# Deformable layer: the grid is added to the 7x7 block's positions by VectorE in place of GpSimd

## The chip, the core and the metric

The kernel runs on one core of a Trainium2 chip. A core has five engines with instruction streams of their own: TensorE (PE in the profile; PEld are its weight loads), VectorE (DVE), ScalarE (ACT), GpSimd (POOL) and SyncE (SP), which here issues most DMAs. They work in parallel and wait for each other by semaphores. Each engine takes its instructions in order, so an instruction that waits holds back all those behind it. The metric is the device time in microseconds of one execution, the median of several.

## What is computed

Four layers on a batch of 8 images of 384 channels, 32x32, all f32, each added to its input: a state-space layer, a deformable convolution, a second state-space layer with an MLP, and a displacement with a small Gaussian filter. The change is in the second. There the 384 normalized channels are split into three blocks of 128, with kernels of 3x3, 5x5 and 7x7. Each block computes offsets by an ordinary convolution, samples its input at the displaced positions with bilinear weights, tap by tap, and mixes channels by a 1x1 convolution:

```python
def deform_block(x, ow, ob, dw, pw, pb, K):
    offsets = conv2d(x, ow, ob, pad)             # 2*K*K channels: dy, dx of each tap
    out = deform_depthwise(x, offsets, dw, K, pad)
    return conv2d(out, pw, pb, 0)
...
    py = gy[None] + ky_k + o_k[:, 0]             # in deform_depthwise, for each tap:
    px = gx[None] + kx_k + o_k[:, 1]             # grid + place of the tap + offset
    acc = acc + sample(py, px) * w_k[None, :, None, None]
```

The 7x7 block has 49 taps, so 98 rows of 1024 positions for each sample. The addition of `gy + ky` and `gx + kx` to these 98 rows is the piece of work that the change touches.

## The kernel before

`tile_net` (line 1725) runs the layers one after another. The deformable layer is `deform_fast` (line 925): it covers about 3060 to 6000 us of the profiled span. If the largest offset, in units of a radius, is too large (`far`), a slower general version (`deform_layer`) computes the layer again; the flag is read at line 1735.

**Units and slots.** For each sample the taps of the three blocks are grouped into sets of up to four (`QUADS`: 3, 7 and 13 sets). Each set is done in two halves of the image rows, which gives 46 units for each sample: units 0 to 5 are the 3x3 block, 6 to 19 the 5x5 block, 20 to 45 the 7x7 block. The loop at line 1007 goes over slots, one unit each, and pipelines four steps of different units in one slot u:

- `positions` (line 1378, DMA at line 1384 on SP) for unit u+4, when it is a first half: it reads the positions of the set's taps from DRAM (`posd`) and broadcasts them over the partitions into `fpyx`. `fpyx` has two buffers, one for the two halves of a set.
- `unit_hats` (line 1389, ScalarE) for unit u+2: bilinear weights in x (`fhx`, lines 1400 and 1406, first half only) and in y (`fhy`, lines 1413 and 1418). Two buffers each.
- `unit_dve` (line 1422, VectorE) for unit u+1: weights the transposed input by the taps (`fxk`, line 1436) and multiplies the hats (`fsm`, line 1453), both from two SBUF operands.
- `unit_pe` (line 1470, TensorE) for unit u: matmuls that accumulate in PSUM (`wacc`, line 1483).

**Everything else goes into the slots by hand.** `block_steps` (line 1058) places the other steps of a block with `put(slot, place, fn)`. A place such as "dve0" is ahead of the slot's units on an engine, "dve1" after them. The order on TensorE, VectorE and ScalarE is the order written out (`manual_schedule`, line 1006). GpSimd and SP are not in that list.

**The 7x7 block's positions.** Its offsets come from a convolution that is split into three parts of matmuls (`fir`, line 1124), in slots 0 to 13 of the sample. `fir_take` (line 1140) puts the even and odd columns into the tile `fpos` (98 x 1024). In slot 14, at "dve0", `fir_end` (line 1151) follows:

```python
def fir_end():
    pos = s["pos"][:used]
...
    nc.gpsimd.tensor_tensor(pos, pos, grid[:used], ALU.add)
    s["posd"] = self.dram.tile([2 * K2, L], F32, name="fposd", tag=f"posd{K}")
    nc.sync.dma_start(out=s["posd"], in_=pos)
```

It takes the largest and smallest offset of each row (lines 1156 and 1157, VectorE), adds the grid in place (line 1158, GpSimd), and stores the sum to DRAM (line 1160, SP). `grid` is a constant of the layer: the setup adds the taps' places to it (line 953). The first set of the 7x7 block, units 20 and 21, has a single tap. Its positions are loaded in slot 16, and its hats are due in slots 18 and 19, its products in 19 and 20. On SP its load stands behind line 1160 and reads what that DMA writes.

The 3x3 and 5x5 blocks add their grid as they take the offsets out of PSUM (line 1184, VectorE) and don't use line 1158.

Of the kernel before, what the change touches and what calls it, by code (L numbers as in the profile page):

```python
# [10 lines left out]
ALU = mybir.AluOpType  # L11
# [80 lines left out]
class Net:  # L92
# [965 lines left out]
    def block_steps(self, b, g, first, put, weights, src, dst):  # L1058
        nc, K = self.nc, KS[g]
        K2, pad = K * K, K // 2  # L1060
        n, st, cols = CONV[K]
        ow, ob, obk, grid, _ = self.f[K]
# [53 lines left out]
        used = width * n  # L1116
# [34 lines left out]
        def fir_end():  # L1151
            pos = s["pos"][:used]
            for e, (op, sign) in enumerate(((ALU.max, 1.0), (ALU.min, -1.0))):
                k = 8 * b + 2 * g + e
                fc = self.far[:used, k : k + 1]
                nc.vector.tensor_reduce(fc, pos, AX.X, op)  # L1156
                nc.vector.tensor_scalar(fc, fc, sign / RAD[K], None, ALU.mult)
            nc.gpsimd.tensor_tensor(pos, pos, grid[:used], ALU.add)  # L1158
            s["posd"] = self.dram.tile([2 * K2, L], F32, name="fposd", tag=f"posd{K}")
            nc.sync.dma_start(out=s["posd"], in_=pos)  # L1160

# [150 lines left out]
        elif g == 1:  # L1312
            t = first[b, 0] - 12
            for i in range(6):
                put(t + i, "pe1", conv, 0, K2 * i // 6, K2 * (i + 1) // 6)
            put(t + 6, "dve0", offsets, 0)
        else:
            t = first[b, 0]
            put(t - 1, "dve1", fir_sum)
            k = 0  # L1320
            for part, pieces in enumerate((4, 5, 5)):
                nw = K * len(FIR[part])
                for i in range(pieces):
                    where = "pe0" if t + k in (first[b, 0], first[b, 1]) else "pe1"
                    put(t + k, where, fir, part, nw * i // pieces, nw * (i + 1) // pieces)
                    k += 1
                put(t + k, "dve0" if part else "act0", fir_take, part)
            put(t + k, "dve0", fir_end)
# [486 lines left out]
```

## Time and profile before

| | |
|---|---|
| device time, median of 3 runs | 9660.02 us (9657.92 to 9662.58) |
| profiled execution | 9658.17 us, of which the span is 9656.4 us |
| mean granted TensorE clock | 0.941 |
| TensorE busy, matmuls | 8491.1 us (88%) |
| VectorE busy | 8114.4 us (84%) |
| ScalarE busy | 6482.8 us (67%) |
| GpSimd busy | 6012.0 us (62%) |
| GpSimd, line 1158 | 8 instructions |
| VectorE, line 1156 (largest and smallest of `fpos`) | 16 instructions, 1.21 us each |
| SP, line 1160 (`fpos` to DRAM) | 8 DMAs of 392 KB |
| SP, line 1384 (`fpyx` from DRAM), sets of four taps | 640 DMAs of 256 KB |
| SP, line 1384, sets of one tap | 24 DMAs of 1024 KB |
| from 3284.8 to 5817.9 us, first to last line 1158: TensorE, VectorE, ScalarE busy | 2270.1, 1944.0, 1896.8 of 2533.1 us |

The span is the time from the first to the last instruction of the profiled execution. Busy shares are averages over layers with different limits, so they don't say what bounds the deformable layer; that is read from who waits for whom there, and from the instructions in order of time. An engine's idle time is put down to what ended it. In this layer GpSimd has no work but line 1158 after its setup, the last of which starts at 3096.7 us.

### The profile page before, as it was taken

How to read it: one execution, taken by the hardware profiler on the slowest of the kernel's cores; microseconds unless marked ns; L12 is line 12 of the kernel's file. 1: busy time of each engine (PE TensorE's matmuls, PEld its weight loads, DVE VectorE, ACT ScalarE, POOL GpSimd, SP SyncE). 2: the span in 40 equal slices, each digit the busy share in tenths (PEclk: the TensorE clock that was granted, in tenths of full speed). 3: DMA queues.
4: the chain of work that ended last, by engine and by line, in shares of the span. 5: the costliest groups of instructions: out<-in, count | busy, mean ns of one | idle time of the engine just before them, and what ended most of it. 6: DMA issues, size and time to landing. Idle time of an engine off the chain costs nothing. (4 is left out here: it accounts for less than half of the span.)

```text
span 9656.4 us, 87414 instructions
## 1 busy us (share of the span) xinstructions
PE 8491.1 (88%) x27891; PEld 4504.2 (47%) x27916; DVE 8114.4 (84%) x8879; ACT 6482.8 (67%) x10148; POOL 6012.0 (62%) x3803
## 2 busy tenths in 40 slices
PE   7898888888886898898898898589999999999987
PEld 3333333333332677677677677233443434434333
DVE  6989999999996678778778778699999999999983
ACT  5666666666663677777777777567777776777750
POOL 6888888888895101101101101599999999999974
PEclk8999999999998999999999999799999999999998
DMA  2211211121121233333333332224333233322336
GB/s 73 81 58 46 83 55 48 61 75 52 49 80 46 71 81 79 87 81 79 87 82 78 87 82 68 85 76 132 95 96 93 89 119 109 96 89 91 110 106 128
DMA packets 566095, 791.97 MB, mean 82 GB/s; under 512 B 244274, under 2 KB 397266, under 8 KB 542072
## 3 DMA queue, kind: packets, MB, share of 16 engines
q1 hardware_dynamic: 513400, 779.99, 27.7%
q10 hardware_dynamic: 52224, 6.30, 0.4%
q8 instruction: 223, 3.65, 0.2%
q14 instruction: 248, 2.03, 0.1%
HBM read 716.49 MB, written 69.66 MB: 81 GB/s over the span
## 5 line engine op out<-in xcount | busy, mean ns | idle before, releaser
L433 POOL TENSOR_TENSOR db<-du,bc 128x1024 f32<-128x1024 f32 x1536 | 3608.3, 2354 | 424.5 <-DVE hs L443 232.0
L443 DVE TENSOR_TENSOR_SCAN da<-da,db 128x1024 f32<-128x1024 f32 x1272 | 2912.5, 2290 | 200.0 <-ACT da L428 149.4
L474 PE MATMUL y<-hs,ident 128*128 128x512 f32 x5184 | 2608.1, 639 | 385.1 <-DVE hs L457 246.1
L428 ACT ACTIVATE da<-dt,na 128x512 f32<-128x512 f32 x3072 | 2120.2, 691 | 915.4 <-DVE hs L457 684.6
L474 PEld LDWEIGHTS y<-hs,ident 128*128 128x128 f32 x5184 | 1020.3, 204 | 1870.9 <-issue 1137.8
L1158 POOL TENSOR_TENSOR fpos<-fpos,fgrid 98x1024 f32<-98x1024 f32 x8 | 244.1, 30508 | 2504.8 <-DVE far L1156 2504.8
L1483 PE MATMUL wacc<-fsm,fxk 128*128 128x221 f32 (+34 forms) x10624 | 1645.1, 313 | 98.8 <-DVE fsm L1453 96.0
L1483 PEld LDWEIGHTS wacc<-fsm,fxk 128*128 128x128 f32 x10624 | 1554.8, 194 | 241.2 <-DVE fsm L1453 162.3
L457 DVE TENSOR_TENSOR hs<-da,bc 128x1024 f32<-128x1024 f32 x1272 | 1557.9, 1225 | 117.2 <-PE y L474 12.8
L1453 DVE TENSOR_TENSOR fsm<-fhy,fhx 128x170 f32<-128x170 f32 (+42 forms) x3216 | 1170.7, 428 | 468.6 <-PE wacc L1483 312.5
L1413 ACT ACTIVATE fhy<-fpyx,cell 128x416 f32<-128x416 f32 (+9 forms) x1280 | 645.5, 576 | 373.3 <-DVE fsm L1453 373.3
L1436 DVE TENSOR_TENSOR fxk<-fxt,fwk 128x1024 f32<-128x1024 f32 (+1 forms) x688 | 787.2, 1180 | 10.1 <-ACT fxt L1226 10.1
L443 DVE TENSOR_TENSOR_SCAN hs<-da,db 128x1024 f32<-128x1024 f32 x264 | 602.4, 2282 | 71.8 <-PE y L474 28.6
L454 POOL TENSOR_TENSOR hs<-hs,bc 128x1024 f32<-128x1024 f32 x264 | 621.8, 2355 | 36.8 <-ACT st L449 36.3
L461 POOL TENSOR_TENSOR hs<-hs 128x512 f32<-128x512 f32 x480 | 609.0, 1269 | 3.6 <-DVE hs L457 3.6
L557 PE MATMUL ps_m<-hid,wm 128*128 128x512 f32 x1152 | 536.8, 611 | 29.0 <-ACT hid L550 24.3
L535 PE MATMUL ps_h<-t,wm 128*128 128x512 f32 x1152 | 539.2, 606 | 14.5 <-DVE x L564 14.4
L1418 ACT ACTIVATE fhy<-fhy,cols 128x1344 f32<-128x1344 f32 (+10 forms) x368 | 530.6, 1442 | 12.0
L401 POOL TENSOR_TENSOR dt<-dt,sp_e 128x512 f32<-128x512 f32 x192 | 243.8, 1270 | 356.6 <-DVE sp_e L393 356.6
L449 ACT COPY st<-da 128x2 f32<-128x2 f32 x624 | 97.8, 157 | 505.5 <-DVE hs L457 504.1
L1135 PE MATMUL ps_off<-fxn,fow 128*98 128x465 f32 (+10 forms) x896 | 386.6, 579 | 0.0
L1400 ACT ACTIVATE fhx<-fpyx,cell 128x544 f32<-128x544 f32 (+8 forms) x640 | 380.0, 666 | 0.0
(203 smaller groups left out, 10086.3 us busy)
## 6 DMA issues: line engine op xcount, KB each, us to landing
bc<-bcd SPq DMA_DIRECT2D x256, 1024.0 KB
fpyx<-fposd SPq DMA_DIRECT2D x640, 256.0 KB
wm<-in_w SPq DMA_DIRECT2D x96, 768.0 KB
x<-x SPq DMA_DIRECT2D x71, 768.0 KB
winr<-in_win SPq DMA_DIRECT2D x192, 192.0 KB
x<-in_x SPq DMA_DIRECT2D x40, 768.0 KB
fpyx<-fposd SPq DMA_DIRECT2D x24, 1024.0 KB
wm<-in_wout SPq DMA_DIRECT2D x48, 384.0 KB
```

Of the source, the lines that this page charges most:

```text
L428: nc.scalar.activation(da[:, i, :], s["dt", j], AF.Exp, scale=na[:, j, n : n + 1])
L433: nc.gpsimd.tensor_tensor(db, du, s["bc"][m][:, 0], ALU.mult)
L443: nc.vector.tensor_tensor_scan(h1, da1, db1, 0.0, ALU.mult, ALU.add)
L454: nc.gpsimd.tensor_tensor(s["hs", m], s["hs", m], c, ALU.mult)
L457: nc.vector.tensor_tensor(hs, s["da", m], c, ALU.mult)
L461: nc.gpsimd.tensor_tensor(hs[:, 0, :], hs[:, 0, :], hs[:, 1, :], ALU.add)
L474: nc.tensor.matmul(s["y"], self.ident, s["hs", m][:, i, :], start=first and i == 0, stop=k == NU - 1 and i == n - 1,)
L535: nc.tensor.matmul(ps, s["w1"][:, k, f * P : (f + 1) * P], s["t"][:, k, :], start=(k == 0), stop=(k == G - 1))
L1413: nc.scalar.activation(hy[:, at : at + (yb - ya) * W], pyx[:, 0, ya * W : yb * W], AF.Abs, bias=bias)
L1436: nc.vector.tensor_tensor(t[:, :n], x, wk[:, j : j + 1, :].to_broadcast([P, n, P]), ALU.mult)
L1453: nc.vector.tensor_tensor(self.sub(sm, at, [(r * w, n), (w, r), (1, w)]), self.sub(hy, hy_at[by] + xa, [(r * W, n), (W, r), (1, w)]), self ...
L1483: nc.tensor.matmul(a[:, ya - 4 * o : yb - 4 * o, xa:xb], k, self.sub(sm, sm_at[by], [(w, yb - ya), (1, w)]), start=False, stop=False,)
```

## The change

The addition in `fir_end` is issued to VectorE's stream instead of GpSimd's. Operands and result are the same: `fpos` plus the first 98 rows of `grid`, in place. In VectorE's order it stands behind the four instructions of lines 1156 and 1157 and ahead of slot 14's products. The store of line 1160 then waits for VectorE. Nothing else is changed.

```diff
@@ -1155,7 +1155,7 @@
                 fc = self.far[:used, k : k + 1]
                 nc.vector.tensor_reduce(fc, pos, AX.X, op)
                 nc.vector.tensor_scalar(fc, fc, sign / RAD[K], None, ALU.mult)
-            nc.gpsimd.tensor_tensor(pos, pos, grid[:used], ALU.add)
+            nc.vector.tensor_tensor(pos, pos, grid[:used], ALU.add)
             s["posd"] = self.dram.tile([2 * K2, L], F32, name="fposd", tag=f"posd{K}")
             nc.sync.dma_start(out=s["posd"], in_=pos)
```

## The prediction

> **What bounds the kernel now.** I read the page first, for the instruction that the change moves. It has three columns after the shapes: busy time in all and mean ns of one; idle time of its engine before it; what ended that idle time.
>
> ```profile
> span 9656.4 us, 87414 instructions
> ...
> L433 POOL TENSOR_TENSOR db<-du,bc 128x1024 f32<-128x1024 f32 x1536 | 3608.3, 2354 | 424.5 <-DVE hs L443 232.0
> ...
> L1158 POOL TENSOR_TENSOR fpos<-fpos,fgrid 98x1024 f32<-98x1024 f32 x8 | 244.1, 30508 | 2504.8 <-DVE far L1156 2504.8
> ```
>
> The reader is to see the odd one: the same operation on the same 1024 elements a partition takes 2354 ns in line 433 and 30508 ns in line 1158. Eight of them, one for each sample, all in the deformable layer. GpSimd has nothing else to do there, so its 244 us cost nothing by themselves. The question is who waits for the result, and what makes it so slow.
>
> Next the waits, in the window of the deformable layer (3000 to 6200 us): total, times, longest. The first answer is SP's own queue, the second that of the engines.
>
> ```profile
> SPq L1160 <- POOL fpos L1158: 300.5, 8, 44.0
> ```
>
> ```profile
> DVE fsm L1453 <- ACT fhy L1418: 153.0, 33, 16.4
> ...
> ACT fhx L1400 <- DMA fpyx<-fposd: 138.0, 8, 17.5
> ...
> PE ps_t L1221 <- DVE frep L1215: 137.0, 10, 16.6
> ```
>
> Eight times SP stands at line 1160, the DMA that writes the finished positions to DRAM, until GpSimd is done. Eight times ScalarE waits some 17 us for positions to come back. VectorE and TensorE show a 16 us wait each, about as often. To see whether that is one stall or several, I read the timeline round the first of them (start, length, engine, line).
>
> ```profile
> 3284.80 2.35 DVE L1436 TENSOR_TENSOR fxk<-fxt,fwk 128x1024 f32<-128x1024 f32 x2
> 3284.84 30.50 POOL L1158 TENSOR_TENSOR fpos<-fpos,fgrid 98x1024 f32<-98x1024 f32 x1 [185.29 <-DVE far L1156]
> ...
> 3305.18 1.05 ACT L1226 COPY fxt<-ps_t 128x512 f32<-128x512 f32 x2
> ...
> 3309.22 3.31 DVE L1453 TENSOR_TENSOR fsm<-fhy,fhx 128x234 f32<-128x234 f32 x12
> ...
> 3312.44 0.69 DVE L1436 TENSOR_TENSOR fxk<-fxt,fwk 128x512 f32<-128x512 f32 x1
> ...
> 3315.37 0.31 SPq L1160 DMA_DIRECT2D fposd<-fpos  x1
> 3318.37 15.38 SPq L1384 DMA_DIRECT2D fpyx<-fposd  x9
> 3323.41 1.15 ACT L1400 ACTIVATE fhx<-fpyx,cols 128x1024 f32<-128x1024 f32 x1 [17.17 <-DMA fpyx<-fposd]
> ...
> 3329.18 1.76 DVE L1453 TENSOR_TENSOR fsm<-fhy,fhx 128x256 f32<-128x256 f32 x3 [16.05 <-ACT fhy L1418]
> 3329.99 2.03 ACT L1413 ACTIVATE fhy<-fpyx,cols 128x384 f32<-128x384 f32 x4
> ...
> 3331.43 1.94 PE L1221 MATMUL ps_t<-ident,frep 128*128 128x128 f32 x8 [16.21 <-DVE frep L1215]
> ```
>
> It is one stall. ScalarE runs out of work at 3306.24 (it starts at 3323.41 after 17.17 us idle), VectorE at 3313.13, TensorE soon after; all wait for the chain add (ends 3315.34), write to DRAM (3.0 us to the next issue), broadcast back (5.0 us more), hats. Asking the waits in a short window round each of the eight gives ScalarE waits of 17.2, 17.5, 17.1, 17.3, 17.4, 17.3, 17.3 and 16.8 us.
>
> Last, busy time by stretch (PE, PEld, DVE, ACT, POOL, then granted clock, DMA share, GB/s):
>
> ```profile
> 3285.00:3313.00 28.00, 24.81 (x180) 24.00 (x180) 28.00 (x63) 16.10 (x24) 28.00 (x1) 0.94 0.00 1
> 3313.00:3331.00 18.00, 2.17 (x13) 1.37 (x13) 1.95 (x5) 7.53 (x11) 2.34 (x1) 0.67 0.48 139
> 3331.00:3360.00 29.00, 22.05 (x105) 16.81 (x105) 23.50 (x43) 27.87 (x42) 0.00 (x0) 0.85 0.48 127
> 3360.00:3400.00 40.00, 35.59 (x214) 34.33 (x215) 38.16 (x84) 34.13 (x47) 0.00 (x0) 0.91 0.36 80
> ```
>
> VectorE is busy for all of 3285 to 3313 while the add hangs, and the add ends 2.2 us after VectorE falls silent (3315.34 less 3313.13), about the length that line 433 has for one. So the add seems to wait until VectorE has no work left, and VectorE has none left because the positions are late: the stall makes itself.
>
> **What the Trainium skill says.** "SBUF — State Buffer", section "Who interferes with whom": VectorE and GpSimd share a pair of ports, and "A DVE instruction with two SBUF inputs contends with a GpSimd instruction that reads SBUF". Lines 1436 and 1453, which fill that stretch, both have two SBUF inputs. The trace agrees, with 30.5 us against 2.35 us, and goes further: the add is not let in between two VectorE instructions either. "GPSIMD Engine Reference", section "Performance versus the Vector engine", gives 2293 ns for an add of 2048 f32 elements on VectorE, so an estimate of 1.15 us for 1024; the trace has 1.22 us for line 1436 (1217 ns on average in 3284 to 5818 us, same types, two SBUF inputs), and I use that.
>
> **The change, part by part.**
>
> Removed: eight GpSimd adds. Nothing else of GpSimd runs in this layer after its setup (last 3096.70, next of another line 6134.19), so that alone is worth nothing.
>
> Added: eight VectorE adds of 98x1024, 1.22 us each. The bounds are 1.15 (the page) and 1.38 (twice the 0.69 us of line 1149, which reads PSUM, for 512). They follow line 1157 in VectorE's written-out order, ahead of lines 1436 and 1453 of the same slot. VectorE is full there, so all of it is on the path: everything up to 3313 shifts by 1.22. It is 9.8 us in all.
>
> Moved: the DMA of line 1160. It now waits for VectorE, at 3284.88 + 1.22 = 3286.1 instead of 3315.37. Behind it in SP's queue stands line 1384 for the first unit of the 7x7 block (unit 20 of the sample). Its data are in DRAM at 3286.1 + 3.0 = 3289.1. Its buffer comes free when ScalarE ends the hats of unit 17, at 3290.00 + 1.89 = 3291.9, or 3293.1 with the shift. Then 5.0 us of transfer: 3298.1. ScalarE needs it at 3306.24. The wait of 17.2 us goes, with 8.1 us to spare. The next load (unit 22) needs the buffer that unit 19's hats free at 3303.7 and has until the hats of unit 22, which move from 3334.37 to some 3318, so it isn't late.
>
> What is late next: ScalarE does the hats of unit 20 (5.7 us in the trace, 3323.41 to 3329.15) from 3306.24 to 3312.0 and one pair of copies (1.05) to 3313.0. The hats of unit 21 then need a buffer that VectorE frees at the end of unit 19's products, 3309.22 + 3.31 + 1.22 = 3313.75. In the trace they start at 3329.99. The gain is 3329.99 less 3313.75, 16.2 us. VectorE itself starts unit 20 at 3314.35 in place of 3329.18 (14.8 earlier), but its wait of 2.9 us for ScalarE at line 1240 comes next (sums, which move with ScalarE), so ScalarE's 16.2 stands. TensorE's wait for line 1215 lies in the same gap and is not counted again.
>
> Sum: the other samples' ScalarE waits differ little, so 137.9 in all (the eight above) less 8 x 1.22 = 9.8 gives 128; by the one worked out in full 8 x 16.2 = 130. I take 129. From the profiled execution, 9658.17 (span 9656.4), that is 9529; its distance to the median of 9660.02 is 1.9 us, within the three runs' spread. I say 9529.
>
> One thing could add to it. The granted clock is 0.67 in the stall and 0.85 and 0.91 in the 70 us after, against 1.00 in stretches from 3400 to 3646. Without a stall it may stay up. In those 70 us VectorE and ScalarE are nearly full (23.5 and 27.9 of 29, then 38.2 of 40), so I cost it at nothing; if half of TensorE's extra time counted (22.05 x 0.15 + 35.59 x 0.09 = 6.5 us), it would be 3.3 us for each sample, 26 us in all.
>
> **The rivals.**
>
> *More than that: the clock.* The stall's cold clock was on the path after it. For it: the 0.85. Against: who is full there. Time: 9529 - 26 = 9503; with all of the 6.5 us, 9477.
>
> *Less: another wait takes its place.* TensorE's busy time is 90% of 2533 us in this layer, and VectorE waits 312.5 us for line 1483 in all (320 waits, none over 5.6 us). If TensorE sets the pace of the units after the pivot, or the positions collide with the next sample's input, which is loaded just after them, half of the gain goes: 9658 - 65 = 9593. Against it: the mean DMA share is 0.32 there, and TensorE, starved from 3315 on, has no backlog at the pivot.
>
> *Nothing: the load isn't released earlier*, because SP still stands behind something else, or the reload is bound by its buffer. Then only the added work remains: 9658 + 10 = 9668. Against it: the buffer's release at 3291.9 is read from the trace, and SP issues nothing between 3271.3 and 3315.37.
>
> *Slower: the price belongs to the operands, not to the engine.* If 98 partitions or this pair of tiles make any engine slow, VectorE takes 30.5 us, in order, with all its products behind it. Unit 19's products then end at 3312.53 + 30.5 = 3343.0 and the pivot moves from 3329.99 to 3343: 13 us for each sample, 9762. It decides from a VectorE add of about 17.5 us on (3329.99 less 3312.53); 20 us would be 9678. Against it: VectorE reads the same fpos tile of 98x1024 in 1.21 us at line 1156, and GpSimd did 98x1024 with one input in 2.85 us at line 953.
>
> **How the numbers follow.** Forecast 0.76 (9529), more 0.10 (9503), less 0.08 (9593), nothing 0.03 (9668), slower 0.03 (9762). The forecast's own range comes from 14.8 to 17.3 us per sample: 9520 to 9540. The range to hold 8 in 10 reaches into the clock's case and half of the way to the halved gain: 9503 to 9562; beyond it lie about half of the cases more and less, and the last two, some 15 in 100. A change under 0.2%, about 19 us, couldn't be told from none. Forecast, more and less lie beyond it on the fast side (0.94), nothing within it (0.03), slower 0.03.
>
> **What would show it.** Right: VectorE has a row for line 1158 of 98x1024 at about 1220 ns; SP's wait at line 1160 falls from 300 us to a few times the shift; ScalarE's wait of line 1400 for fpyx falls from 138 to near 0; VectorE's for line 1418 from 153 to some 25; the interval of two samples' line 1158 falls from 361.9 us (2533.1 / 7) to about 346; the clock stays above 0.9. Wrong: a wait for fpyx of over 5 us left at the start of the 7x7 block, an add longer than 2 us, or a new wait on TensorE of over 5 us in each sample.

## The result, and the profile after

| | before | after |
|---|---|---|
| median, device time | 9661.19 us (9657.92 to 9662.58, 4 runs) | 9529.51 us (9527.39 to 9531.37, 4 runs) |
| span of the profiled execution | 9656.4 us | 9525.6 us |
| ratio, with its 95% interval | | 0.9864 (0.9847 to 0.9881) |

The changed kernel is 131.7 us faster (9661.19 less 9529.51); the forecast was 9529. From its page, with the columns as before, and below it the row of line 1453 on the page before:

```profile
PE 8490.7 (89%) x27916; PEld 4507.3 (47%) x27916; DVE 8122.5 (85%) x8887; ACT 6483.0 (68%) x10148; POOL 5772.1 (61%) x3795
...
L1453 DVE TENSOR_TENSOR fsm<-fhy,fhx 128x170 f32<-128x170 f32 (+42 forms) x3216 | 1171.0, 429 | 344.0 <-PE wacc L1483 317.0
```

```profile
L1453 DVE TENSOR_TENSOR fsm<-fhy,fhx 128x170 f32<-128x170 f32 (+42 forms) x3216 | 1170.7, 428 | 468.6 <-PE wacc L1483 312.5
```

VectorE has eight instructions and 8.1 us of work more (8114.4 to 8122.5), GpSimd 240 us less (6012.0 to 5772.1), and the time fell by neither of these. It is in the row of line 1453: VectorE's idle time before line 1453 was 468.6 us and is 344.0.

The waits of the changed kernel in the deformable layer (3000 to 6200 us; total, times, longest); the second fence is TensorE's, the third SP's queue:

```profile
DVE fsm L1453 <- PE wacc L1483: 317.0, 320, 5.6
...
DVE fsm L1453 <- ACT fhy L1418: 24.0, 25, 4.1
```

```profile
PE ps_t L1221 <- DVE frep L1215: 7.2, 3, 4.7
```

```profile
SPq L1160 <- DVE fpos L1158: 66.4, 8, 14.5
```

VectorE's wait for the hats is 24.0 us in place of 153.0: the eight long ones are gone. ScalarE's wait of 138.0 us for `fpyx` no longer appears at all, and TensorE's for line 1215 fell from 137.0 us to 7.2. SP still stands at line 1160, but only because it comes to that DMA before the offsets are done.

The timeline of the changed kernel at the same place, in the first sample (start, length, engine, line). Its clock reads 6.2 us less than the one before at the same step (line 1156 starts at 3275.96, before at 3282.17), since this execution was already ahead by then:

```profile
3278.60 1.22 DVE L1158 TENSOR_TENSOR fpos<-fpos,fgrid 98x1024 f32<-98x1024 f32 x1
3279.73 2.35 DVE L1436 TENSOR_TENSOR fxk<-fxt,fwk 128x1024 f32<-128x1024 f32 x2
3279.84 0.31 SPq L1160 DMA_DIRECT2D fposd<-fpos  x1
...
3286.86 24.56 SPq L1384 DMA_DIRECT2D fpyx<-fposd  x9
...
3300.11 1.05 ACT L1226 COPY fxt<-ps_t 128x512 f32<-128x512 f32 x2
3301.06 1.16 ACT L1400 ACTIVATE fhx<-fpyx,cols 128x1024 f32<-128x1024 f32 x1
...
3307.67 2.03 ACT L1413 ACTIVATE fhy<-fpyx,cols 128x384 f32<-128x384 f32 x4
```

No bracket stands behind line 1400 any more: ScalarE goes from its copy straight on to the hats of unit 20. The positions were asked for at 3286.86. By an estimate with the 5.0 us of the trace before they were there at 3291.9, some 9 us early. Busy time by stretch (PE, PEld, DVE, ACT, POOL, granted clock, DMA share, GB/s); the first stretch has the times of the stall before, the other two hold the same work as 3331 to 3360 and 3360 to 3400 before, 22.3 us earlier:

```profile
3313.00:3331.00 18.00, 14.54 (x59) 9.90 (x59) 15.53 (x29) 16.97 (x25) 0.00 (x0) 0.91 0.63 172
3308.70:3337.70 29.00, 22.52 (x114) 16.68 (x112) 24.61 (x45) 27.87 (x42) 0.00 (x0) 0.94 0.48 127
3337.70:3377.70 40.00, 35.59 (x238) 34.41 (x239) 39.97 (x88) 36.14 (x52) 0.00 (x0) 1.00 0.39 89
```

The 18 us that held a stall, with VectorE busy for 1.95 us of them, now hold 15.53 us of its work.

**Where the time comes from.** From the first line 1156 to the first line 401 of the next layer it was 2852.0 us (3282.17 to 6134.19) and is 2726.4 (3275.96 to 6002.36): 125.6 us less, 15.7 for each sample. The rest of the 130.8 us between the two spans lies ahead of that (6.2 us, in which the changed instruction has not yet run) and behind the layer (-1.0). So the change itself is worth about 126 us. Two later pairs of medians, below, give 126 and 128 (9653.69 less 9527.26, and 9654.8 less 9527.04).

### The profile page after: what moved, and what is told of

Same layout as the page of the kernel before. It is cut to its first block, busy times and chain, and to the rows that moved or that the text cites. A ratio compares the mean times of both kernels' runs of the same rounds, so it can differ in the third digit from the quotient of the medians.

```text
span 9525.6 us, 87415 instructions
## 1 busy us (share of the span) xinstructions
PE 8490.7 (89%) x27916; PEld 4507.3 (47%) x27916; DVE 8122.5 (85%) x8887; ACT 6483.0 (68%) x10148; POOL 5772.1 (61%) x3795
## 5 line engine op out<-in xcount | busy, mean ns | idle before, releaser
L401 POOL TENSOR_TENSOR dt<-dt,sp_e 128x512 f32<-128x512 f32 x192 | 244.1, 1271 | 2977.7 <-DVE sp_e L393 2977.7
L1453 DVE TENSOR_TENSOR fsm<-fhy,fhx 128x170 f32<-128x170 f32 (+42 forms) x3216 | 1171.0, 429 | 344.0 <-PE wacc L1483 317.0
L535 PE MATMUL ps_h<-t,wm 128*128 128x512 f32 x1152 | 534.5, 601 | 16.6 <-DVE x L564 16.4
L557 PEld LDWEIGHTS ps_m<-hid,wm 128*128 128x128 f32 x1152 | 221.3, 195 | 331.9 <-issue 262.6
```

The source lines that it names most:

```text
L535: nc.tensor.matmul(ps, s["w1"][:, k, f * P : (f + 1) * P], s["t"][:, k, :], start=(k == 0), stop=(k == G - 1))
L557: nc.tensor.matmul(ps, s["w2"][:, f, o * P : (o + 1) * P], s["hid", q][:, f, :], start=(f == 0), stop=(f == 3))
L1453: nc.vector.tensor_tensor(self.sub(sm, at, [(r * w, n), (w, r), (1, w)]), self.sub(hy, hy_at[by] + xa, [(r * W, n), (W, r), (1, w)]), self ...
```

## The experiments

What is to be told apart: that the 30.5 us of the add were a wait for ports that VectorE's two-input instructions held (port theory), against a GpSimd that is slow on these 98 rows (operand theory) or after a long idle time. And whether VectorE is really on the path in slots 14 to 19, as the price of 1.22 us for each add assumes.

**The yardstick.** The changed kernel beside the next three on one chip. Ratios are to the kernel before on the same chip.

> The changed kernel once more, as the yardstick for the three that run beside it. Every theory: 9529 us, 0.986 of the kernel before.

Measured: 9527.26 us (9524.62 to 9534.51), before 9653.69; ratio 0.987 (0.9854 to 0.9886).

**VectorE waits for GpSimd.** To the kernel before, one instruction is added:

```diff
             nc.gpsimd.tensor_tensor(pos, pos, grid[:used], ALU.add)
+            nc.vector.tensor_copy(obk[:used], pos[:, :1])
```

> The kernel before, with the grid still added by GpSimd, and one VectorE instruction more: it reads a column of the sum, so VectorE waits for the add before it goes on. Port theory (VectorE's instructions with two SBUF inputs keep GpSimd out): with VectorE silent the add takes 2.4 us in place of 30.5; VectorE waits about 2.6 us for each sample where the changed kernel spends 1.22, so 9529 + 8 x 1.4 = 9541 us, a wait that makes the kernel 117 us faster than before. Operand theory (98 rows, or this pair of tiles, are slow on GpSimd): the add stays at 30.5 us, VectorE stands still for all of it, and the time is about 9762 us. A GpSimd that is slow because it comes out of a long idle time gives the same 9762.

Measured: 9542.02 us (9539.69 to 9545.38), ratio 0.9884 (0.9868 to 0.9901). The timeline of this kernel, in the first sample:

```profile
3283.66 2.34 POOL L1158 TENSOR_TENSOR fpos<-fpos,fgrid 98x1024 f32<-98x1024 f32 x1 [184.97 <-DVE far L1156]
3286.03 0.31 SPq L1160 DMA_DIRECT2D fposd<-fpos  x1
3286.04 0.15 DVE L1158 COPY fobk<-fpos 98x1 f32<-98x1 f32 x1 [2.32 <-POOL fpos L1158]
3286.11 2.35 DVE L1436 TENSOR_TENSOR fxk<-fxt,fwk 128x1024 f32<-128x1024 f32 x2
```

The same GpSimd instruction, on the same tiles, after the same 185 us of idling, takes 2.34 us when VectorE is silent, in all eight samples (2337 to 2340 ns). Operands and idling are out. A wait of 2.3 us on VectorE, which has no gap there, took 112 us off the time (9653.69 less 9542.02), because it lets in the instruction that everyone waits for 20 us later.

**GpSimd beside the reductions.** GpSimd keeps the add, but does it ahead of line 1156, into a free tile, so that it meets VectorE instructions with one SBUF input only:

```diff
+            out = self.q1.tile([P, L], F32, name="fog2")[:98]
+            nc.gpsimd.tensor_tensor(out, pos, grid[:used], ALU.add)
             for e, (op, sign) in enumerate(((ALU.max, 1.0), (ALU.min, -1.0))):
...
-            nc.gpsimd.tensor_tensor(pos, pos, grid[:used], ALU.add)
...
-            nc.sync.dma_start(out=s["posd"], in_=pos)
+            nc.sync.dma_start(out=s["posd"], in_=out)
```

> GpSimd adds the grid, but ahead of the two reductions of line 1156 and into a tile of its own, so that it runs while VectorE has instructions with one SBUF input (2.7 us of them). Port theory: 2.35 us for each add, done before line 1436 begins, no stall, and VectorE is rid of its 1.22 us: 9529 - 10 = 9519 us, at the most 9529 if the add and the reductions hinder each other. Operand theory: 30.5 us, only begun 2.7 us earlier: 9658 - 8 x 2.7 = 9636 us.

Measured: 9516.56 us (9515.5 to 9517.35), ratio 0.9858 (0.9842 to 0.9874). Its timeline (the added add is line 1819, in a helper at the end of the file, as the added instructions of some kernels below):

```profile
3276.99 1.22 DVE L1156 TENSOR_REDUCE far<-fpos 98x1 f32<-98x1024 f32 x1
3277.11 2.35 POOL L1819 TENSOR_TENSOR fog<-fpos,fgrid 98x1024 f32<-98x1024 f32 x1 [181.05 <-DVE fpos L1149]
...
3278.32 1.21 DVE L1156 TENSOR_REDUCE far<-fpos 98x1 f32<-98x1024 f32 x1
3279.49 0.31 SPq L1160 DMA_DIRECT2D fposd<-fog  x1
```

Neither hinders the other: 2.35 us for the add, 1.22 and 1.21 for the reductions. Who runs beside GpSimd decides, not how busy VectorE is.

The trace of the kernel before shows the same in another way, in the state-space layers. There VectorE's line 457 is a `TENSOR_TENSOR` as well, but one of its inputs, `da`, lies in PSUM (the pool of line 209), and so does that of the scan in line 443:

```profile
1508.16 2.36 POOL L433 TENSOR_TENSOR db<-du,bc 128x1024 f32<-128x1024 f32 x1 [1.17 <-DVE da L443]
1508.18 1.23 DVE L457 TENSOR_TENSOR hs<-da,bc 128x1024 f32<-128x1024 f32 x1
1509.33 2.29 DVE L443 TENSOR_TENSOR_SCAN da<-da,db 128x1024 f32<-128x1024 f32 x1
```

GpSimd's line 433, which reads two tiles in SBUF, overlaps line 457 some 1115 times in this trace, begun before it or after, and then never lasts over 2.40 us, line 457 never over 1.23. So a VectorE instruction with two inputs didn't keep GpSimd out where one of them lay in PSUM.

This kernel, in which GpSimd adds beside the reductions, is also 10.7 us faster than the changed one on the same chip, about the 9.8 us of which VectorE is rid.

**Four more adds.** To the changed kernel:

```diff
             nc.vector.tensor_tensor(pos, pos, grid[:used], ALU.add)
+            for _ in range(4):
+                nc.vector.tensor_tensor(t, pos, grid[:used], ALU.add)
```

> The changed kernel with four further VectorE adds of the same size behind the one of line 1158, into a tile that nobody reads. If VectorE is on the path there, as the prediction costs it, each of the 32 costs its whole 1.22 us: 9529 + 39 = 9568 us. If VectorE has cover there (ScalarE or TensorE set the pace), under 10 us: 9529 to 9539.

Measured: 9566.96 us (9566.12 to 9571.31), ratio 0.9911 (0.9895 to 0.9928). That is 39.7 us over the yardstick for 32 instructions, 1.24 us each; in the list of groups the added instructions (line 1820) have this row:

```profile
L1820 DVE TENSOR_TENSOR fog<-fpos,fgrid 98x1024 f32<-98x1024 f32 x32 | 39.2, 1224 | 1.0
```

Busy 39.2 us, slower by 39.7: nothing of VectorE's work is hidden there.

**GpSimd works, and nobody waits.** To the changed kernel, behind the store, an instruction into an unused tile `t`, of four kinds by sample:

```diff
             nc.sync.dma_start(out=s["posd"], in_=pos)
+            if b % 4 == 0:
+                nc.gpsimd.tensor_tensor(t[:98], pos, grid[:98], ALU.add)
+            elif b % 4 == 1:
+                nc.gpsimd.tensor_scalar(t[:98], pos, 1.0, None, ALU.add)
+            elif b % 4 == 2:
+                nc.vector.tensor_copy(t[:, :1], self.far[:, :1])
+                nc.gpsimd.memset(t, 0.0)
+            else:
+                nc.gpsimd.tensor_tensor(t[:96], pos[:96], grid[:96], ALU.add)
```

> The changed kernel, with a GpSimd instruction beside VectorE's products in each sample, begun when line 1158 is done, whose result nobody uses: samples 0 and 4 the add of 98x1024; 1 and 5 an addition of a constant to 98x1024 (one SBUF input); 2 and 6 a memset of 128x1024 (no input; VectorE does one tiny copy more); 3 and 7 the add of 96x1024. Port theory: the adds of 98 and of 96 rows both last until VectorE has over 2 us without two SBUF inputs, the first of which is line 1240, some 30 us later: 31 to 34 us each; the one with a constant reads SBUF too, so it hangs the same; the memset takes 1 us. Nobody waits, so the time stays at 9529 (up to 9548 if GpSimd, once in, keeps VectorE out for its 2.35 us). Operand theory: 30.5 us for 98 rows, 2.4 us for 96 rows, 2.85 us with a constant.

Measured: 9528.97 us (9526.42 to 9532.86), ratio 0.9867 (0.9851 to 0.9884): no change. GpSimd's timeline for the first four samples, then VectorE's for the end of the first one:

```profile
3284.03 32.67 POOL L1820 TENSOR_TENSOR fog<-fpos,fgrid 98x1024 f32<-98x1024 f32 x1 [186.82 <-DVE fpos L1158]
3628.55 33.03 POOL L1822 TENSOR_SCALAR fog<-fpos 98x1024 f32<-98x1024 f32 x1 [311.86 <-DVE fpos L1158]
3974.11 0.95 POOL L1825 MEMSET fog<- 128x1024 f32 x1 [312.52 <-DVE fog L1824]
4320.01 32.63 POOL L1827 TENSOR_TENSOR fog<-fpos,fgrid 96x1024 f32<-96x1024 f32 x1 [344.95 <-DVE fpos L1158]
```

```profile
3313.73 0.75 DVE L1215 COPY frep<-fxn 128x512 f32<-128x512 f32 x2
3316.26 2.13 DVE L1240 TENSOR_TENSOR fdsb<-fdsb,wacc 128x512 f32<-128x512 f32 x3 [1.79 <-ACT fdsb L1235]
```

98 rows or 96, one SBUF input or two: all hang until VectorE's first hole. It falls silent at 3314.48, and the add ends at 3284.03 + 32.67 = 3316.70, again 2.2 us later. The memset, which reads nothing, takes 0.95 us in the same place. The hang is about as long as in the kernel before (32.7 us and 30.5), and it costs nothing. So the 126 us were not the price of the contention, but of the chain that waited for it.

**One slot later.** In the changed kernel the whole of `fir_end` moves from slot 14 to 15:

```diff
-            put(t + k, "dve0", fir_end)
+            put(t + k + 1, "dve0", fir_end)
```

> The changed kernel with the whole of fir_end (reductions, add, store) one slot later, about 5 us. The prediction's slack of 8.1 us at the reload says no change: 9529 us, within 5. If the positions are as late as they can be, it costs up to 5 us for each sample: 9569.

Measured: 9529.19 us (9525.16 to 9534.71), ratio 0.9865 (0.9848 to 0.9881). Its trace in the first sample:

```profile
3295.26 23.32 SPq L1384 DMA_DIRECT2D fpyx<-fposd  x9
...
3308.08 1.16 ACT L1400 ACTIVATE fhx<-fpyx,cols 128x1024 f32<-128x1024 f32 x1
```

ScalarE begins unit 20's hats 12.8 us after SP issues the load, without a wait; by the 5.0 us for the transfer, 7.8 us are still to spare. So the positions may come a slot later for nothing. Counted from line 1149, the load itself went out only 1.0 us later than in the changed kernel (12.6 us after it, not 11.6), since there it had stood 4 us for its buffer. How far the slack reaches beyond that was not tried.

**The reductions later.** In the changed kernel VectorE's add writes into the free tile, and lines 1156 and 1157 move to the end of slot 19, where VectorE has that hole of 1.8 us:

```diff
-            for e, (op, sign) in enumerate(((ALU.max, 1.0), (ALU.min, -1.0))):
...
-            nc.vector.tensor_tensor(pos, pos, grid[:used], ALU.add)
+            nc.vector.tensor_tensor(out, pos, grid[:used], ALU.add)
...
-            put(t + k, "dve0", fir_end)
+            put(t + k, "dve0", fir_end)
+            put(t + k + 5, "dve1", fir_far)    # the loop over max and min
```

> The changed kernel with its two reductions and two scalings taken out of slot 14 and put at the end of slot 19; VectorE's add writes into a tile of its own, so that the offsets stay whole for them. If VectorE is on the path in slots 14 to 19, the store of the positions and all of VectorE's products there come 2.6 us earlier, and the reductions fill VectorE's wait of 1.8 us for the sums (line 1240), 0.8 us over: gain 1.8 us for each sample, 9529 - 14 = 9515 us. If TensorE or ScalarE set the pace there: 9529, within 5.

> The kernel in which GpSimd adds beside the reductions, once more, on the chip of far_later: 9517 us, level with far_later if that gains what VectorE is rid of.

> The changed kernel once more, as the yardstick of the other runs on this chip: 9528 us.

Measured on one chip: reductions later 9508.20 us (9500.58 to 9513.0), GpSimd beside the reductions 9518.62 (9516.16 to 9524.64), the changed kernel 9527.04 (9519.99 to 9531.24); ratios to the kernel before 0.9847 (0.9833 to 0.986), 0.9862 (0.9847 to 0.9877) and 0.9867 (0.9851 to 0.9882). By the medians moving the reductions gains 18.8 us where 14 were expected, and the two ranges don't overlap. GpSimd beside the reductions gains 8.4 us here; it was expected level with the moved reductions and is 10.4 us behind them. VectorE's timeline with the reductions moved:

```profile
3314.41 1.21 DVE L1156 TENSOR_REDUCE far<-fpos 98x1 f32<-98x1024 f32 x1
...
3315.73 1.21 DVE L1156 TENSOR_REDUCE far<-fpos 98x1 f32<-98x1024 f32 x1
...
3317.71 2.13 DVE L1240 TENSOR_TENSOR fdsb<-fdsb,wacc 128x512 f32<-128x512 f32 x3
...
3324.97 3.71 DVE L1453 TENSOR_TENSOR fsm<-fhy,fhx 128x165 f32<-128x165 f32 x8
```

The wait of 1.79 us at line 1240 is filled, and a wait of 0.6 us that followed at line 1453 is gone with it, which the expectation had left out: 2.4 us in this sample. Over the layer VectorE's waits at these two lines for ScalarE fell from 84.6 to 70.7 us and from 24.0 to 19.1, 18.8 in all. This is the fastest kernel of the study.

**Who gives way when GpSimd was first?** One execution each. To the changed kernel a GpSimd instruction is added that needs only the first scaling of line 1157. It stands behind line 1158 in the program, but GpSimd begins it before VectorE begins line 1158. First with one SBUF input:

```diff
+            nc.gpsimd.tensor_scalar(t, grid, self.far[:98, 8 * b + 4 : 8 * b + 5], None, ALU.add)
```

> The changed kernel with a GpSimd instruction (grid plus a constant per row, 98x1024, one SBUF input, result not used) that begins after the first scaling of line 1157, so some 1.3 us before VectorE's add of line 1158 with its two SBUF inputs. It asks who gives way when GpSimd was first. If the ports are held for a whole instruction, GpSimd takes its 2.85 us and VectorE's line 1158 takes or begins up to 1.6 us later: up to 13 us on the time, 9542. If VectorE is always preferred, GpSimd is broken off and lasts some 33 us, line 1158 keeps its 1.22 us, and the time is 9529.

Measured: 9531.38 us. Its timeline:

```profile
3282.70 2.84 POOL L1819 TENSOR_SCALAR fog<-fgrid,far 98x1024 f32<-98x1024 f32 x1 [184.16 <-DVE far L1157]
...
3283.76 1.22 DVE L1158 TENSOR_TENSOR fpos<-fpos,fgrid 98x1024 f32<-98x1024 f32 x1
3284.89 2.35 DVE L1436 TENSOR_TENSOR fxk<-fxt,fwk 128x1024 f32<-128x1024 f32 x2
```

Neither reading holds: GpSimd's instruction overlaps lines 1158 and 1436 for 1.8 us, and all take their usual time, in each of the eight samples (2.84 us and 1.21 to 1.22). Hence a second kernel, with two SBUF inputs (one tile read twice) and, in odd samples, a second add behind it:

```diff
+            nc.gpsimd.tensor_scalar(t[:, :1], self.far[:98, 8 * b + 4 : 8 * b + 5], 1.0, None, ALU.add)
+            for _ in range(1 + b % 2):
+                nc.gpsimd.tensor_tensor(t, grid, grid, ALU.add)
```

> The changed kernel with GpSimd work beside line 1158 whose result nobody uses: after a one-column instruction that waits for the first scaling of line 1157, an add with two SBUF inputs (grid plus grid, 98x1024) that begins about 1.2 us ahead of VectorE's line 1158; in samples 1, 3, 5 and 7 a second such add right behind it. If what counts is only who began (an instruction under way goes on beside VectorE, one that comes while VectorE is at it stays out), the first adds take 2.4 us, the second ones some 30 us until VectorE has a hole at line 1240, and line 1158 keeps its 1.22 us: 9530 us. If the form of the instruction with one input was what let it pass beside VectorE before, the first adds hang for 33 us too, or line 1158 is held back by about 1 us.

Measured: 9538.93 us. GpSimd in samples 0 and 1, then VectorE in sample 0:

```profile
3280.13 1.89 POOL L1822 TENSOR_TENSOR fog<-fgrid 98x1024 f32<-98x1024 f32 x1
...
3625.62 35.32 POOL L1822 TENSOR_TENSOR fog<-fgrid 98x1024 f32<-98x1024 f32 x2
```

```profile
3280.98 2.12 DVE L1158 TENSOR_TENSOR fpos<-fpos,fgrid 98x1024 f32<-98x1024 f32 x1
```

Now VectorE gives way: line 1158 takes 2.12 to 2.22 us in place of 1.22 and ends 1.1 us after GpSimd's add (3283.10 and 3282.02), so it seems to have its turn when that is done. Eight times 1.0 us would explain most of what this execution has over the changed kernel (9527 to 9530 us), though it is only one. The second add, which comes while VectorE is at it, stays out: 35.32 less 1.89 is 33.4 us. That who began is all that counts, so that VectorE keeps its 1.22 us, failed; of the alternatives named, line 1158 held back by about 1 us came true.

## Why the prediction was right

- **The stall makes itself: shown.** With VectorE silent the add takes 2.34 us, and a hole of VectorE's that comes for another reason ends the hang just so. The mechanism of the Trainium skill ("SBUF — State Buffer", "Who interferes with whom") is the one at work, down to the memset that passes. Only the instruction with one SBUF input that was begun first, and ran beside line 1158, doesn't fit what the page says there.
- **The waits are one stall: right.** ScalarE's wait went from 138.0 us to nothing, VectorE's from 153.0 to 24.0 and TensorE's from 137.0 to 7.2 with the one release. The sign put down for SP was too low: its wait at line 1160 lost GpSimd's eight adds and gained VectorE's (300.5 - 244.1 + 9.8 is 66.2, measured 66.4), but 56 us of it had come before the add began, and they stay.
- **The added work, 1.22 us on the path: right.** 1.216 us in the trace after (1214 to 1217 ns), and 1.24 us a piece on the time by the four more adds.
- **The reload's slack of 8.1 us: right in kind, a little small.** It is about 9 us, since ScalarE comes to unit 20 1.0 us later than I put it (3301.06 plus the 6.2 us between the executions is 3307.3, not 3306.24): VectorE's shift of 1.22 us reaches it through the hats of unit 17. I had counted it there (3293.1) and left it out at 3306.24.
- **What is late next, ScalarE's hats of unit 21: right.** Put at 3313.75, found at 3307.67, which is 3313.87 with the same 6.2 us. The gain at that place is 16.1 us, against 16.2; over the eight samples it is 15.7 to 16.4, 129.6 in all.
- **The sum: 129 predicted, about 126 in the layer.** The interval of two samples' line 1158 went from 361.9 to 346.2 us ((5701.9 - 3278.6) / 7), 15.7 for each sample. So some 4 us of the 129.6 are lost between unit 21's hats and the next sample's reductions. VectorE's wait for TensorE at line 1453 grew by as much, from 312.5 to 317.0 us; that these are the same microseconds is not shown. That the forecast met the median within 1 us is in part luck: some 5 us of the difference between the two executions lie outside the stretch that the change touches. In the executions profiled here the layer's first memset starts anywhere between 3056.9 and 3065.3 us.
- **The clock, costed at nothing: right.** Over the same work it is 0.94 and 1.00 in place of 0.85 and 0.91. Yet from unit 21's hats to line 1259 both executions take 24.1 us in the first sample (3329.99 to 3354.07, 3307.67 to 3331.75).
- **The rival on the slower side,** that any engine is slow on these operands, fell with line 1158 itself: VectorE needs 1.22 us for it, and GpSimd 2.34 when VectorE is silent.

## What to carry to other kernels

An instruction that lasts ten times as long as its like may be waiting, not working, as here: look at what runs beside it on the engine that it may share ports with, and what its end coincides with. An engine with nothing else to do is no free place for a step whose result is due soon; what its delay costs is read from who waits for the result, and is nothing if nobody does. If such a step must stay on GpSimd, two ways worked here: begin it where VectorE has reductions, or make VectorE wait for it. And once the stall was gone, the next gain lay in moving other work off the same path, into a wait that was already there.

## What the runs showed of the hardware that was not expected

In these traces a GpSimd instruction that reads SBUF, and comes second, does not get in between two VectorE instructions with two SBUF inputs: it stood for 28 to 31 us behind some sixty of them. The pairs of copies of line 1215 among them, with one input (128x512, 0.42 us each), were no way in either, though the reductions are; whether that is for the kind of the copy or only because it is short isn't shown. In the reverse order it depends on the GpSimd instruction: an add with two SBUF inputs (one tile read twice) that was first held VectorE's add back by 1.0 us, while one with a single SBUF input and a value for each row ran beside it and line 1436 for 1.8 us, and none was longer. Yet begun second, an addition of a constant, with a single input too, hung for 33.0 us like the others. Why order and form combine in this way stays open.
